# Reordering the small steps beside a deformable convolution: bursts last in their step, sums and statistics earlier, eleven gathers

## The chip, the cores and the metric

The kernel runs on one core of a Trainium2 chip. The metric is the device time of one execution in microseconds; where several runs are given, their median. The engines are named as the profile names them: PE is TensorE (PEld its weight loads), DVE is VectorE, ACT is ScalarE, POOL is GpSimd (here it only issues gathers), SP is SyncE (here it only issues transfers).

## The reference, cut to what matters

Eight images of 256 channels and 64 x 64 points in f32 go through two layers. Each is x + layer(group norm(x)).

```python
def layer0(x):                       # local attention, 4 heads, 3x3 windows
    q, k, v = split(einsum('oc,bchw->bohw', w_qkv, x))
    attn = softmax(sum_d(q * patches(k)))             # 9 weights a head and point
    kernel = grouped_1x1(w_kg, qkv) + b_kg            # 9 more weights, generated
    out = alpha * sum_k(kernel * patches(v)) + beta * sum_k(attn * patches(v))
    return einsum('oc,bchw->bohw', w_proj, out)

def layer1(x):                       # modulated deformable 3x3 convolution
    om = conv3x3(x, w_off) + b_off                    # 18 offsets and 9 masks a point
    v = mask * bilinear(x at the 9 shifted positions) # 4 corners for each
    return einsum('bckhw,ock->bohw', v, w)
```

## The kernel before

A *chunk* is 8 rows of an image, 512 points; an image has 8. The kernel writes out the order of every instruction by hand (`manual_schedule`) for PE, ACT, DVE and POOL; each engine's queue runs in that order. SP's transfers are ordered by what they depend on.

**Slots.** The convolution of layer 1 runs in slots, one for each of the 9 kernel positions of a chunk: 72 an image, 576 in all. Its work is in blocks of 128 points, four a slot. POOL gathers a block's four corners for 256 channels (`gather`, line 764) into one of GATHERS = 10 buffers; ACT scales the first corner (`scale`, 780); DVE adds the other three with three instructions (`sum_corners`, 788). PE transposes the four blocks (`transposes`, 815), ACT copies the result out (818), and PE multiplies it with the weights a slot later (`product`, 832). The product of the 9 slots of a chunk stays in one accumulator `po`, which has a single buffer. After the last of them DVE adds it to the residual r (`finished`, 843) and SP stores it. `ahead(i)` scales blocks i+8 and i+9, sums blocks i+6 and i+7 and issues two gathers; it is called twice a slot. In the last image it issues them four blocks later (LAST_GATHERS = 6).

**Steps.** Everything else is cut into 73 steps an image, which generators yield: two for the first norm, 7 for each of the 8 chunks of attention, 6 that finish the attention and its norm, and 9 for `prepare`, which writes the table to gather from, computes offsets (649), positions (682 to 715) and, for the next image, the first norm's statistics (258). Steps of image b+1 lie beside the slots of image b. Before the first slot, image 0's 73 steps and 6 more run alone; after that each slot is joined by one step (73 for 72 slots), until all are done about 78 slots before the end. A slot's order is: transposes, `ahead`, the product of the slot before, the step, the final sums if the product was a chunk's last, `ahead`.

**A chunk's attention.** In `attention` (550), `a_` is the current chunk and `d` the one before, which is finished beside it. The seven steps are:
1. `spread_weights` of d (475; DVE multiplies the four results, 483), both halves of `q` (276, ACT copies 284);
2. `k` (308) of 10 rows of 66 columns, written in two pieces of 4 rows;
3. `products` (64 small multiplies, 346; DVE masks, 354), first `weighted` half of d (516);
4. `logits` (365 to 374), `keys(1)` of d (498), `generated` (381), `softmax_1` (412, 413, ACT's exponential 414);
5. `v(0)` (308), second `weighted` half, `turned` (398; DVE adds the bias, 402), `softmax_2` (419 to 421), `normed` for the next chunk (228);
6. `v(1)`, `project(0)` (528) and its `add` (539), `softmax_3` (428 to 450);
7. `project(1)` and `add`, `second_stats` (543), `weights` (462), `keys(0)`.

PSUM tiles of the steps come from a ring of four (`psum_a`, 189): each new tile takes the place of the one four before it, once that has been read. `Norm` (195) aggregates statistics on DVE (199) and multiplies the means on PE (201) in one step; `ready` (209) does the variance and the root in the next.

Of the kernel before, what the change touches and what calls it, by code (L numbers as in the profile page):

```python
# [17 lines left out]
P = 128  # L18
C = 256
# [31 lines left out]
GATHERS = 10  # L51
LEAD = SCALE_AHEAD + GATHERS
LAST_GATHERS = 6
# [5 lines left out]
def preact_kernel(ctx: ExitStack, tc: tile.TileContext, a: dict, out: bass.AP):  # L59
# [77 lines left out]

    kt = const.tile([P, NT, R + 2, WP], F32, tag="k", name="k")
    vt = const.tile([P, NT, TC, KT, KT], F32, tag="v", name="v")


    w_effT = const.tile([P, NT, HEADS, KK], F32, tag="w_effT", name="w_effT")
    nc.vector.tensor_scalar(bkg, bkg, alpha, None, ALU.mult)
    with (
        tc.tile_pool(name="prep", bufs=1) as prep,
        tc.tile_pool(name="prep_ps", bufs=1, space=PSUM) as prep_ps,
    ):
        ps = prep_ps.tile([P, NT, HEADS, KK], F32, tag="eff", name="eff")
        for ct in range(NT):
            for h in range(HEADS):  # L150
                for i in range(2):
                    nc.tensor.matmul(
                        ps[:, ct, h, :],
                        w_qkv[h // 2][:, 2 * (h % 2) + i, ct * P : (ct + 1) * P],
                        w_kgT[:, 2 * h + i, :],
                        start=(i == 0),
                        stop=(i == 1),
                    )
        for ct in range(NT):
            nc.vector.tensor_scalar(  # L160
                w_effT[:, ct], ps[:, ct], alpha, None, ALU.mult
            )

        zero = prep.tile([P, ES], F32, tag="zero", name="zero")
        nc.vector.memset(zero, 0.0)
        tables = []  # L170
        for i in range(min(2, B)):
            t = dram.tile([ENTRIES, ES], F32, tag=f"table{i}", name=f"table{i}")
            tables.append(t)
            nc.sync.dma_start(t[:WP], zero[:WP])
            for o in range(H * WP, ENTRIES, P):
                n = min(P, ENTRIES - o)
                nc.sync.dma_start(t[o : o + n], zero[:n])
# [6 lines left out]
    wp = ctx.enter_context(tc.tile_pool(name="wp", bufs=NC + 3))  # L184
# [7 lines left out]
    class Norm:  # L192


        def __init__(self, stats, name):
            self.name = name
            mv = p1.tile([P, NT, 2], F32, tag="mv", name=f"mv_{name}")
            for ct in range(NT):
                nc.vector.bn_aggr(mv[:, ct, :], stats[:, ct].rearrange("p c s -> p (c s)"))
            ps = psum_a(f"gn_{name}")  # L200
            nc.tensor.matmul(ps[:, 0:NT], gmat, mv[:, :, 0], start=True, stop=True)
            self.gn = gn = p2.tile([P, 2, NT], F32, tag="gn", name=f"gn_{name}")
            nc.vector.tensor_copy(gn[:, 0, :], ps[:, 0:NT])
            self.d = d = p1.tile([P, NT], F32, tag="gnd", name=f"gnd_{name}")
            nc.vector.tensor_sub(d, mv[:, :, 0], gn[:, 0, :])
            nc.vector.tensor_mul(d, d, d)
            nc.vector.tensor_add(d, d, mv[:, :, 1])
# [44 lines left out]
    stats0: dict = {}  # L252

    def first_stats(b, c):
        if c == 0:
            stats0[b] = p2.tile([P, NT, NC, 6], F32, tag="stats0", name=f"stats0_{b}")
        for ct in range(NT):
            nc.vector.bn_stats(
                stats0[b][:, ct, c, :], image[:, ct, c * N : (c + 1) * N]
            )  # L260

    class Attention:
# [38 lines left out]
        def keyed(self, which, i, to):  # L301

            for lo, hi in [(0, 2)] * (self.c == 0 and i == 0) + [(2 + 4 * i, 6 + 4 * i)]:
                for m in range(NT):
                    ps = psum_a(f"ps{'qkv'[which]}_{self.u}_{lo}_{m}")
                    o = which * C + m * P
                    for ct in range(NT):
                        nc.tensor.matmul(  # L308
                            ps[:, : (hi - lo) * WP],
                            w_qkvT[:, ct, o : o + P],  # L310
# [4 lines left out]
                    to(m, lo, hi, ps)  # L315

        def k(self, i):
            self.keyed(
                1,
                i,  # L320
                lambda m, lo, hi, ps: nc.scalar.copy(  # L321
                    kt[:, m, lo:hi, :].rearrange("p r w -> p (r w)"), ps[:, : (hi - lo) * WP]
                ),
            )

        def v(self, i):
            self.keyed(
                2,
                i,
                lambda m, lo, hi, ps: nc.scalar.copy(vt[:, m, :, lo:hi, :], tiled(ps, hi - lo)),  # L330
            )

        def products(self):


            self.qk = qk = p1.tile([P, NB, NT, 2, NK], F32, tag="qk", name=f"qk_{self.u}")
            for jj in range(NB // 2):
                both = [psum_a(f"qk_{self.u}_{jj}_{h}") for h in range(2)]
                for ct in range(NT):
                    for j in range(2):  # L340
                        for t in range(2):
                            o = 2 * (2 * jj + j) + t
                            for h in range(2):
                                r = slice(64 * h, 64 * h + 64)
                                n = (2 * j + ct) * NK
                                nc.tensor.matmul(  # L346
                                    both[h][64 * t : 64 * t + 64, n : n + NK],
                                    self.qt[r, ct, o * T * T : (o + 1) * T * T],
                                    kt[r, ct, :, T * o : T * o + KT],
                                    start=True,  # L350
                                    stop=True,
                                )
                for h in range(2):
                    nc.vector.tensor_mul(  # L354
                        qk[:, 2 * jj : 2 * jj + 2, :, h, :],
                        both[h][:, : 4 * NK].rearrange("p (j c k) -> p j c k", j=2, c=NT),
                        near_k.unsqueeze(1).unsqueeze(1).to_broadcast([P, 2, NT, NK]),
                    )
# [17 lines left out]
        def generated(self):  # L376

            ps = psum_a(f"gen_{self.u}")
            n = HEADS * KK
            for ct in range(NT):  # L380
                nc.tensor.matmul(
                    ps[:n],
                    w_effT[:, ct].rearrange("p h k -> p (h k)"),
                    window(self.xn, ct, 4),
                    start=(ct == 0),
                    stop=(ct == NT - 1),
                )
            self.gs = gs = p1.tile([P, N], F32, tag="gs", name=f"gs_{self.u}")[:n]
            nc.scalar.copy(
                gs.rearrange("p (t y x) -> p y t x", y=T, x=T),  # L390
                ps[:n].rearrange("p (y t x) -> p y t x", y=T, x=T),
            )

        def turned(self):
            ps = psum_a(f"gt_{self.u}")
            n = HEADS * KK
            for j in range(NB):
                nc.tensor.transpose(
                    ps[:, j * n : (j + 1) * n], self.gs[:, j * P : (j + 1) * P], ident[:n, :n]
                )  # L400
# [3 lines left out]
                ps[:, : NB * n].rearrange("p (j k) -> p j k", j=NB),  # L404
# [145 lines left out]
    def attention(b):  # L550

        xt = image
        gn = Norm(stats0.pop(b), f"0_{b}")
# [5 lines left out]
        d = None  # L559
        for c in range(NC):  # L560
            a_ = Attention(b, c, xn, stats)
            if d:
                d.spread_weights()
            a_.q(0)
            a_.q(1)
# [3 lines left out]
            yield None  # L569
            a_.products()  # L570
# [3 lines left out]
            a_.logits()  # L574
# [4 lines left out]
            a_.softmax_1()  # L579
            a_.carry_k()  # L580
            yield None
            a_.v(0)
            if d:
                d.weighted(1)
            a_.turned()
            a_.softmax_2()
# [3 lines left out]
            a_.v(1)  # L590
            if d:
                d.add(0, d.project(0))
            a_.softmax_3()
# [4 lines left out]
            a_.weights()  # L598
            a_.keys(0)
            yield None  # L600
            d = a_
# [9 lines left out]
        d.second_stats()  # L611
        yield None
        gn = Norm(stats, f"1_{b}")
# [3 lines left out]
    def prepare(b, gn):  # L617
# [24 lines left out]
        def offsets(c, xn):  # L642
# [14 lines left out]
            om = p1.tile([P, N], F32, tag="gs", name=f"om_{b}_{c}")  # L657
# [134 lines left out]
    def ahead(i):  # L792
# [4 lines left out]
        first = (B - 1) * BLOCKS  # L797
        for n in (i + LEAD, i + LEAD + 1):
            if n < first:
                gather(n)  # L800

        for n in (i + LEAD, i + LEAD + 1):
            if n - GATHERS + LAST_GATHERS >= first:
                gather(n - GATHERS + LAST_GATHERS)

# [48 lines left out]
    with tc.manual_schedule(engines=ordered):  # L854
# [4 lines left out]
        while done < STEPS + STEPS_AHEAD:  # L859
# [15 lines left out]
        for n in range(B * SLOTS + 1):  # L875
            if n < B * SLOTS:
                transposes(*divmod(n, SLOTS))
                ahead(NB * n)
            last = None
            if n > 0:  # L880
                b, h = divmod(n - 1, SLOTS)
                product(b, h)
                if h % KK == KK - 1:
                    last = b, h // KK
            while (done - STEPS - STEPS_AHEAD) * SLOTS < (n + 1) * STEPS:
                next(steps, None)
                done += 1
            if last:
                finished(*last)
            if n < B * SLOTS:  # L890
# [79 lines left out]
```

## Time and profile before

| | us |
|---|---|
| median of 9 runs | 5189.31 (5174.74 to 5207.84) |
| the profiled execution | 5177.06 |
| its span | 5175.3 |
| DVE busy, 0 to 340 / 340 to 4690 / 4690 to the end | 177.7 / 3603.1 / 403.6 |
| PE busy, the same | 273.4 / 4038.9 / 414.9 |
| ACT waits for gathers (line 780 <- DMA) | 434.6 in all, 226.4 in the middle part, 208.2 in the last |
| DVE waits for ACT's scaling (788 <- 780) | 395.5 |

The costliest groups of the page are, with busy us and mean ns: the corner sums on DVE (788) 2799.5 and 479, the convolution's product on PE (832) 2149.1 and 610, the scaling on ACT (780) 1080.6 and 510, the transposes on PE (815) 695.2 and 284. An f32 matmul counts as two instructions (4608 for 2304 products), and a mean of one runs past the start of the next, so times here are taken from start to start. `us, times, longest` follow each pair of engine and releaser in the view of waits. PEclk is the granted clock of PE in tenths.

### The profile page before, as it was taken

The numbers are of one execution on the slowest core, as the hardware profiler recorded it, in microseconds if no ns is written. First come the engines' busy times: TensorE is split into PE (matmuls) and PEld (weight loads), VectorE is DVE, ScalarE is ACT, GpSimd is POOL, SyncE is SP. The second block draws the span as 40 slices with busy tenths as digits, with TensorE's granted clock in tenths as the row PEclk, the third lists the DMA queues.
The fourth block names the chain that finished last, engine by engine and source line by source line (L and its number), as shares of the span: only waits on it lengthen the run. The fifth ranks groups of instructions, "written<-read, shape, count | busy, mean of one in ns | idle before, by whom it ended". The sixth has DMA issues, their size and how long they took to land. (4 is left out here: it accounts for less than half of the span.)

```text
span 5175.3 us, 79716 instructions
## 1 busy us (share of the span) xinstructions
PE 4727.2 (91%) x26592; PEld 2634.4 (51%) x26592; DVE 4184.3 (81%) x10071; ACT 2362.3 (46%) x5184; POOL 3177.1 (61%) x2310
## 2 busy tenths in 40 slices
PE   6979999999999999899998999899999999998888
PEld 4545554555545555455554555445554455544443
DVE  4558787888878888788888888878888887877887
ACT  2334444444444444444444444445444444444544
POOL 0027666666656666566665766757666666666776
PEclk9989999999999999999999999999999999999999
DMA  2058778877787777977779787888878877788998
GB/s 91 21 181 281 266 272 297 305 273 261 273 313 282 273 261 263 332 265 275 277 262 327 270 281 263 285 303 290 273 257 306 300 275 261 272 294 318 380 377 336
DMA packets 476840, 1422.60 MB, mean 275 GB/s; under 512 B 46910, under 2 KB 114750, under 8 KB 476300
## 3 DMA queue, kind: packets, MB, share of 16 engines
q0 software_dynamic: 331776, 1208.11, 66.3%
q1 hardware_dynamic: 141902, 204.27, 11.1%
q10 hardware_dynamic: 2750, 5.12, 0.3%
q8 instruction: 210, 3.44, 0.3%
q14 instruction: 202, 1.65, 0.1%
HBM read 1280.19 MB, written 137.13 MB: 274 GB/s over the span
## 5 line engine op out<-in xcount | busy, mean ns | idle before, releaser
L764 POOL DMA_INDIRECT g<-table,idx x2304 | 3174.6, 1378 | 1976.5 <-DVE s L788 651.0
L788 DVE SCALAR_TENSOR_TENSOR s<-g,wt,s 128x256 f32<-128x256 f32 x6912 | 2799.5, 479 | 404.2 <-ACT s L780 395.5
L832 PE MATMUL po<-vt,w_conv 128*128 128x512 f32 x4608 | 2149.1, 610 | 94.1 <-DVE r L843 94.1
L832 PEld LDWEIGHTS po<-vt,w_conv 128*128 128x128 f32 x4608 | 858.5, 197 | 977.0 <-issue 871.5
L780 ACT ACTIVATE s<-g,wt 128x256 f32<-128x256 f32 x2304 | 1080.6, 510 | 492.2 <-DMA g<-table,idx 434.6
L815 PE MATMUL pt<-ident,s 128*128 128x128 f32 x4608 | 695.2, 284 | 110.4 <-DVE s L788 74.2
L815 PEld LDWEIGHTS pt<-ident,s 128*128 128x128 f32 x4608 | 520.0, 143 | 408.8 <-ACT vt L818 117.5
L818 ACT COPY vt<-pt 128x512 f32<-128x512 f32 x1152 | 610.9, 582 | 119.8 <-PE pt L815 119.4
L276 PE MATMUL psq<-xn,w_qkvT 128*128 128x512 f32 x512 | 284.3, 705 | 91.4 <-DVE wk L483 88.2
L284 ACT COPY q<-psq 128x512 f32<-128x512 f32 x128 | 75.0, 586 | 509.0 <-PE psq L276 509.0
L649 PE MATMUL om<-xn,w_off 128*32 128x512 f32 x2304 | 295.4, 610 | 10.9 <-DVE pos L682 10.8
L308 PE MATMUL psv<-xn,w_qkvT 128*128 128x264 f32 (+1 forms) x1088 | 260.4, 384 | 0.0
L354 DVE TENSOR_TENSOR qk<-qk,near_k 128x400 f32<-128x400 f32 x256 | 129.2, 567 | 161.2 <-PE qk L346 161.2
L308 PE MATMUL psk<-xn,w_qkvT 128*128 128x264 f32 (+1 forms) x1088 | 245.5, 379 | 0.0
L308 PEld LDWEIGHTS psv<-xn,w_qkvT 128*128 128x128 f32 x1088 | 201.6, 192 | 83.2 <-issue 50.6
L276 PEld LDWEIGHTS psq<-xn,w_qkvT 128*128 128x128 f32 x512 | 109.5, 224 | 263.2 <-DVE wk L483 146.1
L528 PE MATMUL proj<-acc,w_projT 128*128 128x512 f32 x512 | 238.2, 592 | 0.7 <-ACT acc L523 0.7
L308 PEld LDWEIGHTS psk<-xn,w_qkvT 128*128 128x128 f32 x1088 | 201.7, 190 | 60.0 <-issue 20.8
L330 ACT COPY v<-psv 128x320 f32<-128x320 f32 (+1 forms) x272 | 110.7, 419 | 255.1 <-PE psv L308 255.0
L321 ACT COPY k<-psk 128x264 f32<-128x264 f32 (+1 forms) x272 | 101.2, 372 | 214.8 <-PE psk L308 214.5
L523 ACT COPY acc<-av 128x512 f32<-128x512 f32 x128 | 74.8, 585 | 254.7 <-PE av L516 254.4
L483 DVE TENSOR_TENSOR wk<-wk,near 100x512 f32<-100x512 f32 x256 | 158.8, 683 | 32.3 <-PE wk L475 32.3
(89 smaller groups left out, 3295.2 us busy)
## 6 DMA issues: line engine op xcount, KB each, us to landing
table<-ts SPq DMA_DIRECT2D x384, 176.0 KB
g<-table,idx POOLq DMA_INDIRECT x2304
x<-in_x_dram SPq DMA_DIRECT2D x64, 512.0 KB
x<-x SPq DMA_DIRECT2D x64, 512.0 KB
r<-x SPq DMA_DIRECT2D x64, 512.0 KB
out_dram<-r SPq DMA_DIRECT2D x64, 512.0 KB
w_conv<-in_w_conv_dram ACTq DMA_DIRECT2D x1, 2304.0 KB
w_qkv<-in_w_qkv_dram ACTq DMA_DIRECT2D x2, 384.0 KB
```

Of the source, the lines that this page charges most:

```text
L276: nc.tensor.matmul(ps, w_qkvT[:, ct, m * P : (m + 1) * P], window(self.xn, ct, 4), start=(ct == 0), stop=(ct == NT - 1),)
L308: nc.tensor.matmul(ps[:, : (hi - lo) * WP], w_qkvT[:, ct, o : o + P], self.xn[:, ct, lo:hi, :], start=(ct == 0), stop=(ct == NT - 1),)
L354: nc.vector.tensor_mul(qk[:, 2 * jj : 2 * jj + 2, :, h, :], both[h][:, : 4 * NK].rearrange("p (j c k) -> p j c k", j=2, c=NT), near_k.unsq ...
L483: nc.vector.tensor_mul(wk.rearrange("p (t n) -> p t n", n=T * T), ps[:NK].rearrange("p (t n) -> p t n", n=T * T), near.unsqueeze(1).to_bro ...
L528: nc.tensor.matmul(ps, w_projT[:, ct, m * P : (m + 1) * P], self.acc[:, ct].rearrange("p (t y x) -> p y t x", y=T, x=T), start=(ct == 0), ...
L649: nc.tensor.matmul(ps[32 * g : 32 * g + 32, :], w_off[:, ct, k, :], window(xn, ct, k), start=(n < 4), stop=(n >= KK * NT - 4),)
L764: nc.gpsimd.indirect_dma_start(out=g, out_offset=None, in_=tables[b % 2], in_offset=bass.IndirectOffsetOnAxis(ap=found[b, c][0][:, j, k : ...
L780: nc.scalar.activation(s, g[:, 0:C], AF.Copy, scale=w[:, 0:1])
L788: nc.vector.scalar_tensor_tensor(s, g[:, q * C : (q + 1) * C], w[:, q : q + 1], s, ALU.mult, ALU.add)
L815: nc.tensor.transpose(pt[ct][:, j, :], s[:, ct * P : (ct + 1) * P], ident)
L818: nc.scalar.copy(v[:, ct, :], pt[ct].rearrange("p b n -> p (b n)"))
L832: nc.tensor.matmul(po[:, m, :], w_conv[:, ct, k, m * P : (m + 1) * P], v[:, ct, :], start=(k == 0 and ct == 0), stop=(k == KK - 1 and ct = ...
```

## The change

- The steps of a chunk are put together anew: (1) `q(1)`, then spreading; (2) `k`, then the first weighted half; (3) `keys(1)`, `generated`, the first half of the products; (4) `v(0)`, the second half of the products, `normed`; (5) `v(1)`, `turned`, the second weighted half, `logits`, `softmax_1`; (6) `project(0)`, `add`, `keys(0)`, `softmax_2`, `softmax_3`; (7) `project(1)`, `add`, statistics, `q(0)` of the next chunk, `weights`.
- `k` is computed for 64 columns, all 8 rows in one tile of 512; its border is set to zero once. The generated weights use all 128 columns of the array (zeros in w_effT); their tile now shares a buffer with `wsb` and `om`.
- In a chunk's last slot the second `ahead` and the final sums stand before the step.
- The aggregation of a norm's statistics stands at the end of the step that completes them; the means (`means`) follow in the next.
- GATHERS is 11, in the last image too. Before the first slot 73 steps run, not 79; the 6 are made up over the first image's slots.

```diff
-GATHERS = 10
+GATHERS = 11
-LAST_GATHERS = 6
...
+    nc.gpsimd.memset(kt, 0.0)
...
+    w_effT = const.tile([P, NT, P], F32, tag="w_effT", name="w_effT")
+    nc.vector.memset(w_effT, 0.0)
...
-    wp = ctx.enter_context(tc.tile_pool(name="wp", bufs=NC + 3))
+    wp = ctx.enter_context(tc.tile_pool(name="wp", bufs=NC + 2))
...
+        if c == NC - 1:
+            norm0[b] = Norm(stats0[b], f"0_{b}")
...
+        def k(self, m):
+            for lo, hi in [(0, 2)] * (self.c == 0) + [(2, R + 2)]:
+                ps = psum_a(f"psk_{self.u}_{lo}_{m}")
+                for ct in range(NT):
+                    nc.tensor.matmul(
+                        ps[:, : (hi - lo) * W],
+                        w_qkvT[:, ct, C + m * P : C + (m + 1) * P],
+                        self.xn[:, ct, lo:hi, 1 : W + 1],
...
         for c in range(NC):
-            a_ = Attention(b, c, xn, stats)
+            a_.q(1)
             if d:
                 d.spread_weights()
-            a_.q(0)
-            a_.q(1)
             yield None
             a_.k(0)
             a_.k(1)
-            yield None
-            a_.products()
             if d:
                 d.weighted(0)
             yield None
-            a_.logits()
             if d:
                 d.keys(1)
                 d.carry_v()
             a_.generated()
-            a_.softmax_1()
-            a_.carry_k()
+            a_.products(0)
             yield None
             a_.v(0)
-            if d:
-                d.weighted(1)
-            a_.turned()
-            a_.softmax_2()
+            a_.products(1)
+            a_.carry_k()
             if c + 1 < NC:
                 xn = normed(xt, gn, c + 1)
             yield None
             a_.v(1)
+            a_.turned()
+            if d:
+                d.weighted(1)
+            a_.logits()
+            a_.softmax_1()
+            yield None
             if d:
                 d.add(0, d.project(0))
+            a_.keys(0)
+            a_.softmax_2()
             a_.softmax_3()
             yield None
             if d:
                 d.add(1, d.project(1))
                 d.second_stats()
-            a_.weights()
-            a_.keys(0)
+            d = a_
+            if c + 1 < NC:
+                a_ = Attention(b, c + 1, xn, stats)
+                a_.q(0)
+            d.weights()
             yield None
-            d = a_
...
         d.second_stats()
+        gn = Norm(stats, f"1_{b}")
         yield None
-        gn = Norm(stats, f"1_{b}")
+        gn.means()
         yield None
         yield gn.ready()
...
-        first = (B - 1) * BLOCKS
-        for n in (i + LEAD, i + LEAD + 1):
-            if n < first:
-                gather(n)
-
-        for n in (i + LEAD, i + LEAD + 1):
-            if n - GATHERS + LAST_GATHERS >= first:
-                gather(n - GATHERS + LAST_GATHERS)
+        gather(i + LEAD)
+        gather(i + LEAD + 1)
...
-        while done < STEPS + STEPS_AHEAD:
+        while done < STEPS:
...
         for n in range(B * SLOTS + 1):
+            last = None
+            if n > 0 and n % KK == 0:
+                last = divmod(n // KK - 1, NC)
             if n < B * SLOTS:
                 transposes(*divmod(n, SLOTS))
                 ahead(NB * n)
-            last = None
+                if last:
+                    ahead(NB * n + 2)
             if n > 0:
-                b, h = divmod(n - 1, SLOTS)
-                product(b, h)
-                if h % KK == KK - 1:
-                    last = b, h // KK
-            while (done - STEPS - STEPS_AHEAD) * SLOTS < (n + 1) * STEPS:
+                product(*divmod(n - 1, SLOTS))
+            if last:
+                finished(*last)
+
+            goal = (n + 1) * STEPS + min(n + 1, SLOTS) * STEPS_AHEAD
+            while (done - STEPS) * SLOTS < goal:
                 next(steps, None)
                 done += 1
-            if last:
-                finished(*last)
-            if n < B * SLOTS:
+            if n < B * SLOTS and not last:
                 ahead(NB * n + 2)
```

## The prediction

> **What bounds the kernel now.** I read the busy shares first, then who waits for whom, then the order in time on two engines. From the page:
>
> ```profile
> PE 4727.2 (91%) x26592; PEld 2634.4 (51%) x26592; DVE 4184.3 (81%) x10071; ACT 2362.3 (46%) x5184; POOL 3177.1 (61%) x2310
> PEclk9989999999999999999999999999999999999999
> ```
>
> TensorE works 91% of the span at almost full clock; VectorE is second at 81%. The span has three parts: up to 340 us (no slots), 340 to 4690 (slots with steps beside them), 4690 to the end (slots alone). What TensorE waits for in the middle part is the whole question:
>
> ```profile
> PE psq L276 <- DVE wk L483: 88.2, 49, 2.2
> PE po L832 <- DVE r L843: 88.0, 40, 4.5
> PE gn L201 <- DVE mv L199: 49.5, 14, 5.6
> PE pt L815 <- DVE s L788: 29.2, 79, 6.5
> PE pt L815 <- ACT vt L818: 22.1, 12, 3.2
> ```
>
> (Engine, line, releaser: us, times, longest.) The first three are what the change moves: queries behind spreading, the product of a new chunk behind the final sums, the means behind the aggregation. A wait also costs clock. Busy time by stretch, with the granted clock after POOL's column:
>
> ```profile
> 2000.00:2005.00 5.00, 4.71 (x7) 2.02 (x8) 4.40 (x10) 0.58 (x1) 4.39 (x3) 0.66 0.85 293
> 2005.00:2010.00 5.00, 5.00 (x19) 2.70 (x18) 2.49 (x6) 3.15 (x7) 3.78 (x5) 1.00 0.81 261
> ```
>
> At 2000 us TensorE had just waited 2.21 us; the clock is 0.66 in the next 5 us. So a wait is priced with its slow stretch.
>
> Then the order in time, TensorE (start, duration) and VectorE:
>
> ```profile
> 2000.29 5.40 PE L276 MATMUL psq<-xn,w_qkvT 128*128 128x512 f32 x8 [2.21 <-DVE wk L483]
> 2020.49 1.09 PE L815 MATMUL pt<-ident,s 128*128 128x128 f32 x8
> 2024.85 1.04 PE L498 MATMUL vk<-ident,v 128*100 128x128 f32 x8
> 2210.75 0.59 PE L201 MATMUL gn<-mv,gmat 128*128 128x2 f32 x2 [5.58 <-DVE mv L199]
> ```
>
> ```profile
> 1994.81 4.82 DVE L788 SCALAR_TENSOR_TENSOR s<-g,wt,s 128x256 f32<-128x256 f32 x12
> 1999.55 2.48 DVE L483 TENSOR_TENSOR wk<-wk,near 100x512 f32<-100x512 f32 x4
> 2205.36 4.83 DVE L788 SCALAR_TENSOR_TENSOR s<-g,wt,s 128x256 f32<-128x256 f32 x12
> 2210.09 0.60 DVE L199 BATCH_NORM_AGGREGATE mv<-stats 128x2 f32<-128x48 f32 x2
> ```
>
> A slot's transposes and products cost TensorE 4.36 us (2020.49 to 2024.85); its twelve corner sums cost VectorE 4.82. In steps without a wait, start to start on TensorE: queries 3.44 for two, spreading 1.05, keys of the window 3.56, small products 1.6, a weighted half 1.1, the turned keys (vk) 0.97, generated 1.84, a value half 1.8, a projection 1.72, weights 0.44. One chunk is 7 slots of 4.36 plus 23.5, so 54 us; VectorE's is 7 x 4.82 plus 15.9 of step work plus 1.29 for final sums every 9 slots, so 51 to 52. Chunks really take about 59.3 (queries at 2333 and 2632, five chunks apart, are 299 us apart, over 59 each). TensorE is the bound by a margin of 3 us in 54: **VectorE is next, close behind**.
>
> **Part by part**, against the profiled execution (span 5175.3, time 5177.06; the median shown is 5189.31, 12 higher; I add the sum to the median). The middle part holds images 1 to 7, 56 chunks.
>
> *Queries before spreading.* 88.2 us of waiting go. Their slow stretches too: the queries' matmuls there are busy 251.7 us for 448, 0.562 each; unhindered (94.42 to 97.97 in the first part) eight take 3.55, 0.444 each; 0.118 x 448 = 53. So -141. What is late next: the fourth spreading product needs the fourth buffer of the ring of four, which ScalarE empties of the query (0.586 us) while TensorE does three spreadings (0.8); with a hand-over about 0.2 x 56 = +11 (between 0 and one copy, +33).
>
> *Final sums before the step.* 88.0 us of waiting go; 28 of the 40 are above 2 us, each with 53/49 = 1.1 us of slow clock as above: 31. So -119. What comes back: in a chunk's last slot VectorE now does twelve corner sums (4.82), the sums on r (1.29), then the step. Below I count by which step they meet.
>
> *Statistics forward.* The wait of 5.58 at 2210.75 looks free to take. But the twelve corner sums of 2205.36 to 2210.1 stand ahead of the aggregation, and the transposes behind gn need the last six of them. With the aggregation earlier, gn starts at 2206 and the transposes stop till 2210.7. The 49.5 us mostly change their name: about 0.6 to 0.9 gained in each of 14, -10. (Bounds: 0 and -50 with clock.)
>
> *Small products, softmax and statistics spread.* TensorE's work only changes place. VectorE's step work per chunk was 2.5, 0, 2.0, 3.7, 2.0 to 2.5, 3.5, 1.9; it becomes 2.5, 0, 1.0, 2.1, 4.0 (bias, logits, first softmax), 4.45 (add, rest of the softmax), 1.9. Steps five and six cost TensorE 7.8 and 7.0 with their slots, VectorE 8.8 and 9.3: it falls 3.3 us behind. How much TensorE feels: step four ends in a burst whose products VectorE must multiply, so both meet at zero there. VectorE then needs 1.0, 1.1 (normed), 4.8, 4.0, 4.8 before it has finished the corner sums that the transposes of step seven need: 15.8 against TensorE's 14.8 plus 0.4 of first transposes, a wait of 0.7. Step six's 4.45 and 4.8 more: 25.1 against 24.2, 1.0. Later steps catch up (step two has no VectorE work). So 1.7 a chunk, **+95** (bounds: 0 if my zero is off by a microsecond, and 3.3 a chunk, +185).
> With final sums in the slot, the same count with 1.29 and six corner sums moved ahead gives an extra wait of about 2.7, 1.0, 0, 0.6, 1.2, 2.1, 3.6 us as they meet steps one to seven: 1.6 on average. 43 of the 56 fall on attention steps: 69, with 6 for the others **+75**. Three in seven are above 2 us: 18 x 1.1 = **+20** of slow clock. Behind a late VectorE, ScalarE's exponential holds the scales and the evacuation of pt; counted as above, pt is empty 1.5 us before it is needed, so nothing.
>
> *Keys in 512 columns.* 8 instructions of 0.43 (3.44) for 16 (3.56): -7. ScalarE: 2 x 0.585 for 4 x 0.372, off the path. *Generated and turned at full width:* 1.84 to 1.72 and 0.37 to 0.44, -3. *Bursts apart:* before, products and weighted stood together; one more small-tile visit a chunk. The gap between po and qk at 2017.8 is about 0.1, so +10. Together 0. [...]
> [...]
>
> *Eleven gathers, eleven in the last image too.* Middle: ScalarE waits 226.4 us there for gathers, but TensorE feels 22.1 of it (pt <- vt); between 0 and -22 (up to +10 if tables written at the same time land later), taken -15. Last part: DMA share 0.92, 356 GB/s, while 398 occurs at 2075: at best -50; r and the output share the engines with five more gathers, 7 us each for 8 chunks, at worst +55. Taken -10.
>
> *Six steps fewer ahead of the first slot.* gather(0) waits for the last positions (338.43) before as after. The first transposes come at 365.5 now, since VectorE, ScalarE and TensorE do four attention steps first; without them some 16 us earlier, but those 17 us of TensorE work then lie in image 0's slots. Nothing, +-10. Memsets (about 1.2 and 0.5 us by rows L136, L131) lie in the load.
>
> **Sum.** -141 +11 -119 -10 +95 +75 +20 +0 -15 -10 = **-94**: 5189 - 94 = **5095** (profile: about 5083).
>
> **Rivals.**
> 1. *VectorE keeps up.* If its delay is absorbed, only the 11 comes back: -141 -119 -10 +11 -25 = -284, **4905**. For it: pt <- s is only 29.2 us now, and VectorE's idle in the middle part is 4350 - 3603 = 747. Against: it runs without a pause from 2043.4 to 2068.
> 2. *Given back entirely*, the waits only renamed as with gn: returns near 5 us a chunk, **5190**, within 0.3%, about what a measurement of this kernel can tell from no change.
> 3. *The softmax lump decides: slower.* The delay of steps five and six is felt whole, 3.3 a chunk instead of 1.7 (+90), with a slow stretch each (56 x 1.1 = +62): **5247**. It decides once new stalls and their clock exceed 295/56 = 5.3 us a chunk. For it: both engines have nearly equal loads, and steps five and six hold 8.4 of 15.9. Against: step two gives VectorE 4 us to recover.
>
> **Chances.** Forecast 0.55 (4990 to 5160), rival 1 0.20, rival 2 0.12 (a little of it still faster), rival 3 0.13. Faster 0.77, same 0.10, slower 0.13. The range 4900 to 5205 takes in half of rival 1 and all of rival 2.
>
> **What would show it.** psq <- wk gone and psq's mean near 610 ns: the first step right. po <- r smaller but alive, at 2 to 3.6 us: the second. gn <- mv gone with new waits of 4 to 5 us at pt beside it: the third. pt <- s grown from 29 to above 100 us, VectorE without idle from step five to one, idle in steps two to four: the fourth. If pt <- s stays near 30, rival 1 holds. I am wrong if ScalarE or the gathers become what VectorE waits for (s <- s above 336), or if the last part is longer than 485.

## The result, and the profile after

The changed kernel takes **5217.15 us** (median of 10 runs, 5203.05 to 5236.81); the kernel before 5184.22 (31 runs). The ratio is **1.0065** (95% interval 1.0051 to 1.0079): 0.65% slower, clear of the noise, where 0.98 was forecast. The profiled execution has a span of 5205.5 us.

Its page, the busy time of the engines:

```profile
PE 4776.9 (92%) x26080; PEld 2577.3 (50%) x26080; DVE 4177.1 (80%) x10072; ACT 2372.4 (46%) x5056; POOL 3329.7 (64%) x2311
```

TensorE has 512 matmul instructions fewer to do and is busy 50 us longer; its mean granted clock is 0.966 against 0.967, so over the whole span no slow clock was gained. It went from the queries, as meant (the page's rows before and after), but the rows of the projection rose from 592 to 616 ns in the mean and those of the convolution's product from 610 to 617:

```profile
L276 PE MATMUL psq<-xn,w_qkvT 128*128 128x512 f32 x512 | 284.3, 705 | 91.4 <-DVE wk L483 88.2
L286 PE MATMUL psq<-xn,w_qkvT 128*128 128x512 f32 x512 | 244.0, 601 | 1.6 <-DVE xn L235 1.6
```

What TensorE waits for between 340 and 4690 us:

```profile
PE pt L820 <- DVE s L799: 117.1, 128, 11.7
PE po L837 <- DVE r L848: 75.9, 42, 3.4
PE qk L354 <- ACT vk L508: 30.9, 16, 3.5
PE proj L533 <- ACT acc L528: 20.9, 7, 3.4
PE ptab L640 <- DVE xn L235: 17.2, 14, 2.5
PE w L467 <- DVE wts L455: 16.3, 7, 3.4
```

psq and gn are gone from the list, as the change meant. But all lines together are 308 us, against 314 before: **the waits changed their names**. po <- r, which was 88, stands at 76; qk, proj and w are new.

Where in a chunk the time lies is seen from the start of each slot's first transposes. Mean length of a slot by its place in the chunk, images 1 to 6 (place 0 holds the final sums of the chunk before, place 1 begins the new chunk's product):

| place | 0 | 1 | 2 | 3 | 4 | 5 | 6 | 7 | 8 | sum |
|---|---|---|---|---|---|---|---|---|---|---|
| before | 9.42 | 10.43 | 7.12 | 9.47 | 7.87 | 8.77 | 8.11 | 8.58 | 8.76 | 78.5 |
| changed | 9.74 | 10.65 | 8.24 | 8.84 | 8.17 | 8.44 | 8.56 | 8.26 | 8.21 | 79.1 |

Places 0 and 1, which the new order of final sums was to shorten, are longer, and place 2 by most. And the first image: slot 0 begins 15.8 us earlier than before (349.7 against 365.5), slot 72 begins 16.6 us later (1005.4 against 988.8).

One last slot shows what keeps po. VectorE and then TensorE, in order of time; step seven lies in the slot that ends at 2583.45, the final sums in the next:

```profile
2580.03 7.21 DVE L799 SCALAR_TENSOR_TENSOR s<-g,wt,s 128x256 f32<-128x256 f32 x18
2587.16 1.28 DVE L848 TENSOR_TENSOR r<-po,r 128x512 f32<-128x512 f32 x2
```

```profile
2583.45 0.60 PE L820 MATMUL pt<-ident,s 128*128 128x128 f32 x4
2584.52 0.83 PE L820 MATMUL pt<-ident,s 128*128 128x128 f32 x4 [0.47 <-DVE s L799]
2588.49 6.25 PE L837 MATMUL po<-vt,w_conv 128*128 128x512 f32 x8 [3.14 <-DVE r L848]
```

VectorE comes late out of the softmax and has 18 corner sums in a row before it: 6 left over from the slot before the last, then the last slot's 12, six of which the change has put here. Only then does it free po. TensorE waits 3.14 us, and its next product takes 6.25 instead of 3.70, at a granted clock of 0.59. This is one of the worst cases: of the 42 products after such a wait 18 are lengthened, by 2.0 us in the mean, 36 us in all; the other 24 take 3.70.

The longest waits at pt between two images come from elsewhere: there VectorE waits for a load of x, and its corner sums stand behind that.

```profile
3487.59 1.29 DVE L266 BATCH_NORM_STATS2 stats<-x 128x6 f32<-128x512 f32 x2 [9.05 <-DMA x<-in_x_dram]
3490.99 1.09 PE L820 MATMUL pt<-ident,s 128*128 128x128 f32 x4 [5.03 <-DVE s L799]
```

These waits of VectorE for x are 76.1 us in the middle part, against 22.0 before.

### The profile page after: what moved, and what is told of

Read it like the earlier page. It is cut to its first block, busy times and chain, and to the rows that moved or that the text cites. A ratio compares the mean times of both kernels' runs of the same rounds, so it can differ in the third digit from the quotient of the medians.

```text
span 5205.5 us, 78551 instructions
## 1 busy us (share of the span) xinstructions
PE 4776.9 (92%) x26080; PEld 2577.3 (50%) x26080; DVE 4177.1 (80%) x10072; ACT 2372.4 (46%) x5056; POOL 3329.7 (64%) x2311
## 4 chain that ended last, share of the span: by engine, by line
PE 42%; DVE 34%; DMA 17%; issue 4%; ACT 2%; POOL 1%; SPq 0%; DVEq 0%; ACTq 0%; POOLq 0%
DVE s L799 19%; PE po L837 17%; DMA g<-table,idx 11%; PE pt L820 4%; PE psk L315 4%; DMA x<-in_x_dram 4%; PE psv L332 3%; PE psq L286 2%; PE qk L354 2%; PE om L660 2%; DMA table<-ts 2%; DVE xn L235 2%; PE wk L480 2%; DVE by L373 2%; PE gen L388 1%
## 5 line engine op out<-in xcount | busy, mean ns | idle before, releaser
L775 POOL DMA_INDIRECT g<-table,idx x2304 | 3326.0, 1444 | 1855.1 <-DVE s L799 643.3
L837 PE MATMUL po<-vt,w_conv 128*128 128x512 f32 x4608 | 2174.7, 617 | 102.1 <-DVE r L848 102.1
L820 PE MATMUL pt<-ident,s 128*128 128x128 f32 x4608 | 711.5, 286 | 146.2 <-DVE s L799 132.6
L533 PE MATMUL proj<-acc,w_projT 128*128 128x512 f32 x512 | 250.5, 616 | 26.3 <-ACT acc L528 26.3
L286 PE MATMUL psq<-xn,w_qkvT 128*128 128x512 f32 x512 | 244.0, 601 | 1.6 <-DVE xn L235 1.6
L315 PE MATMUL psk<-xn,w_qkvT 128*128 128x512 f32 (+1 forms) x576 | 238.1, 558 | 0.3
L322 ACT COPY k<-psk 128x512 f32<-128x512 f32 (+1 forms) x144 | 78.0, 552 | 266.3 <-PE psk L315 266.3
L646 ACT COPY ts<-ptab 88x512 f32<-88x512 f32 x192 | 106.6, 584 | 167.2 <-DMA table<-ts 133.7
L533 PEld LDWEIGHTS proj<-acc,w_projT 128*128 128x128 f32 x512 | 98.8, 197 | 150.5 <-issue 108.2
L660 PEld LDWEIGHTS om<-xn,w_off 128*32 128x32 f32 x2304 | 74.9, 111 | 186.6 <-issue 160.6
```

The costliest lines, as they stand in the source:

```text
L286: nc.tensor.matmul(ps, w_qkvT[:, ct, m * P : (m + 1) * P], window(self.xn, ct, 4), start=(ct == 0), stop=(ct == NT - 1),)
L315: nc.tensor.matmul(ps[:, : (hi - lo) * W], w_qkvT[:, ct, C + m * P : C + (m + 1) * P], self.xn[:, ct, lo:hi, 1 : W + 1], start=(ct == 0), ...
L533: nc.tensor.matmul(ps, w_projT[:, ct, m * P : (m + 1) * P], self.acc[:, ct].rearrange("p (t y x) -> p y t x", y=T, x=T), start=(ct == 0), ...
L660: nc.tensor.matmul(ps[32 * g : 32 * g + 32, :], w_off[:, ct, k, :], window(xn, ct, k), start=(n < 4), stop=(n >= KK * NT - 4),)
L775: nc.gpsimd.indirect_dma_start(out=g, out_offset=None, in_=tables[b % 2], in_offset=bass.IndirectOffsetOnAxis(ap=found[b, c][0][:, j, k : ...
L820: nc.tensor.transpose(pt[ct][:, j, :], s[:, ct * P : (ct + 1) * P], ident)
```

## The experiments

Eighteen runs in five sets, each on a chip of its own. The chips fall into two kinds. Where the result above and the third set were measured, the kernel before takes about 5180 us; on the other four chips it takes 5535 to 5553, and a slot without steps takes 7.4 to 8.0 us instead of 5.6 to 5.8. Ratios are to the kernel before on the same chip; I call the chips quick and slow. The changed kernel itself was not run beside the third set, so what is said there against it is across two chips of the quick kind (kernel before: 5184 and 5179 us).

The theories: **A**, parts of the change cost, each by itself (the order of the last slot, the six steps, spreading's wait for the query's copy); **B**, the new grouping with VectorE's delay after steps five and six is the cost; **C**, eleven gathers hold up other transfers.

**First set: one part undone** (slow chip, no run of the changed kernel beside).

*undo_steps*: 79 steps ahead again.

```diff
-        while done < STEPS:
+        while done < STEPS + STEPS_AHEAD:
...
-            goal = (n + 1) * STEPS + min(n + 1, SLOTS) * STEPS_AHEAD
-            while (done - STEPS) * SLOTS < goal:
+            while (done - STEPS - STEPS_AHEAD) * SLOTS < (n + 1) * STEPS:
```

> The changed kernel with 79 steps run before the first slot again; all else as changed. Kernel before 5184, changed kernel 5217. Theory A (parts of the change cost, each by itself: six steps moved beside the slots of image 0, scales that stand before their gathers have landed in a chunk's last slot, the spreading products' wait for the query's copy): slot 72 of the changed kernel comes 17 us later than before although its first slot comes 16 us earlier, so this gives some 15 us back, about 5200. Theory B (the new grouping of the steps is the cost, VectorE's delay after steps five and six): the six steps cost what they cost anywhere, within 3 us of 5217.

*undo_final*: final sums and second ahead behind the step.

```diff
-                if last:
-                    ahead(NB * n + 2)
...
-            if last:
-                finished(*last)
...
-            if n < B * SLOTS and not last:
+            if last:
+                finished(*last)
+            if n < B * SLOTS:
```

> The changed kernel with the final sums and the second ahead of a chunk's last slot behind the step again, as before. Theory A: in last slots ScalarE's wait for gathers falls from 147 to some 30 us and the waits of qk for vk and of proj for acc (52 us) go; po behind r returns to about 90. Net gain 25 to 45, about 5180. Theory B: the final sums are no loss where they stand, and their old place costs the wait of po again: 5217 to 5240.

*sums_early*: only the second ahead behind the step.

```diff
-                if last:
-                    ahead(NB * n + 2)
...
-            if n < B * SLOTS and not last:
+            if n < B * SLOTS:
                 ahead(NB * n + 2)
```

> The changed kernel with only the second ahead of a chunk's last slot behind the step again; the final sums stay before the step. Theory A: the scales are what is early, not the sums: as good as or better than the run with both behind, 5165 to 5180, with po behind r well under 76 us. If the place of the final sums themselves costs, it stays near 5217. Theory B: within 5 us of 5217.

*undo_gathers*: 10 gathers, 6 in the last image (the diff of the change, backwards).

> The changed kernel with 10 gathers, 6 in the last image, as before. Theory A: eleven gathers are a gain, 15 us of it in the last image (the lag on the kernel before falls from 46 to 31 us there), so this is about 5232 or more. Rival C (a deeper queue of gathers holds up the loads of x and the table writes: VectorE's wait for x rose from 22 to 76 us in the middle part, ScalarE's for table writes from 92 to 132): the slots between images get 3 to 5 us shorter each, about 5200.

| | ratio | interval |
|---|---|---|
| undo_steps | 1.0160 | 1.0139 to 1.0181 |
| undo_final | 1.0152 | 1.0133 to 1.0171 |
| sums_early | 1.0139 | 1.0117 to 1.0160 |
| undo_gathers | 1.0153 | 1.0132 to 1.0175 |

The times can't be set against 5217 and lie within each other's intervals, so no verdict by time. The trace shows the waits: po <- r (340 to 4900 us) is 63.0 us in undo_steps, which has the new order, 136.2 in undo_final and 5.1 in sums_early. With the new steps the old place of the final sums makes TensorE wait longer than the new; without the second ahead in front of them the wait is gone. Theory C finds nothing in undo_gathers: VectorE still waits 58.9 us for loads of x between 340 and 4690 (60.1 in undo_steps).

**Second set: the changed kernel as measure** (slow chip).

> The changed kernel itself, as the common measure: the chip of the last four runs needs 7.4 to 8.0 us for a slot without steps, where the chip of the kernel before and of the changed kernel needs 5.7 to 5.8, so those four can't be set against 5217. Both theories: 1.0065 of the kernel before if the chip moves gathers as fast as the first (5.7 us a slot in the last part), some 1.015 if it is as slow as the second.

> 79 steps before the first slot, all else as changed. Theory A: 15 us less than the changed kernel on the same chip, since slot 72 came 17 us late with 73. Theory B: within 3 us of it.

> Only the second ahead of a chunk's last slot behind the step again; final sums stay early. Theory A (scales that stand before their gathers have landed hold ScalarE, and with it vk, acc and the products that need them): ScalarE's wait for gathers in last slots falls from 147 to below 60 us, the waits of qk for vk and proj for acc (52 us in the middle part) go; 25 to 45 us less than the changed kernel. Theory B: within 5 us of it.

*q_in_seven*: both halves of q in step seven.

```diff
         a_.q(0)
+        a_.q(1)
         for c in range(NC):
-            a_.q(1)
...
                 a_.q(0)
+                a_.q(1)
             d.weights()
```

> The changed kernel with both halves of q in step seven, so that step one is spreading alone and its four results find tiles of the ring that were read long before. Theory A: the four spreading products take 1.05 us again instead of 1.84 (the fourth waited for the query's copy), 0.75 x 56 chunks = 42 us less work on TensorE; but step one leaves TensorE 5.4 us beside VectorE's 7.3 and step seven becomes 10.3, so a part comes back as waits of pt for s: 10 to 35 us less than the changed kernel. Theory B (VectorE is the bound in steps five to one): no gain, pt behind s grows by as much as the spreading gains, within 5 us.

| | us | ratio | interval |
|---|---|---|---|
| after_again | 5636.15 | 1.0180 | 1.0156 to 1.0203 |
| undo_steps_2 | 5628.25 | 1.0164 | 1.0139 to 1.0188 |
| sums_early_2 | 5599.98 | 1.0105 | 1.0084 to 1.0127 |
| q_in_seven | 5652.70 | 1.0212 | 1.0185 to 1.0240 |

sums_early_2 is 36 us below the changed kernel, the expected size, intervals apart (the fourth set shows that the reason expected there, early scales, was not it). The six steps are not told from nothing here. In q_in_seven the four spreadings take 1.05 us again (1.77 in the changed kernel, median of 64), as expected, and yet it is not faster: pt <- s is 193 us against 182, qk <- vk 55 against 44. There B was right: the waits for VectorE and ScalarE grew by about what the spreadings gained.

**Third set: parts alone** (quick chip).

*q_alone* and *sums_alone* are the kernel before with one part each (the changed kernel has only one half of q ahead of the spreading in step one, q_alone has both):

```diff
-            if d:
-                d.spread_weights()
             a_.q(0)
             a_.q(1)
+            if d:
+                d.spread_weights()
```

```diff
+            if last:
+                finished(*last)
             while (done - STEPS - STEPS_AHEAD) * SLOTS < (n + 1) * STEPS:
                 next(steps, None)
                 done += 1
-            if last:
-                finished(*last)
```

> The kernel before, with one part of the change alone: in step one both halves of q come ahead of the spreading. Theory A: the 88 us that psq waits for wk and the slow clock behind them (53) go; the fourth spreading product then waits some 0.75 us for the query's copy (42 us in all), and a part comes back as waits for VectorE: 0.985 to 0.995 of the kernel before. Theory B (VectorE is the bound in these slots, its delay only changes its name): 0.995 to 1.0, pt behind s up by 60 us or more.

> The kernel before, with another part alone: the final sums stand before the step, the second ahead stays behind it. Theory A: po behind r (88 us and 31 us of slow clock) goes nearly whole, since VectorE reaches the sums after six corner sums (2.45 us) and the product of the slot's own accumulator, and nothing is early on ScalarE: 0.985 to 0.995. Theory B: VectorE waits for the product instead (1.9 us each) and gives it back to pt: 0.998 to 1.003.

*grouping_alone* is the changed kernel with undo_steps, undo_final and undo_gathers together; *best_after* the changed kernel with undo_steps and sums_early.

> The new steps alone (with the keys in 512 columns, the full width and the statistics forward); the order of a chunk's last slot, the 79 steps ahead and the gathers as before. Theory A: the steps themselves are no loss, slots two to eight of a chunk are as fast or faster: 0.990 to 1.002. Theory B (the grouping is what makes the changed kernel slow): as slow as the changed kernel, 1.005 or more.

> The changed kernel with 79 steps ahead and with the second ahead behind the step; final sums early. Theory A: both gains add, 30 to 55 us below the changed kernel, so 0.996 to 1.001 of the kernel before on a chip with quick gathers, some 1.009 on one with slow ones. Theory B: no more than 10 us below the changed kernel.

| | us | ratio | interval |
|---|---|---|---|
| q_alone | 5094.97 | 0.9833 | 0.9809 to 0.9856 |
| sums_alone | 5138.55 | 0.9922 | 0.9901 to 0.9942 |
| grouping_alone | 5234.87 | 1.0105 | 1.0084 to 1.0126 |
| best_after | 5061.55 | **0.9770** | 0.9748 to 0.9793 |

Two parts of the change are gains alone; the grouping alone is a loss, as B said; and the grouping, the early sums and the gathers, with the second ahead and the six steps put back, **beat both kernels** by 118 and about 155 us, far more than the 30 to 55 that I expected against the changed kernel. In grouping_alone po <- r is the largest wait of all (136.6 us from 340 to 4690), with the sums behind the heavy steps; with the sums early, in best_after, the grouping does no harm that shows. That it gains anything is not shown: the two parts alone multiply to 0.9756, which lies within best_after's interval. In best_after, over the same stretch:

```profile
PE pt L820 <- DVE s L799: 129.8, 165, 4.2
PE proj L533 <- ACT acc L528: 20.5, 7, 3.5
PE ptab L640 <- DVE xn L235: 19.4, 14, 3.0
PE w L467 <- DVE wts L455: 16.7, 7, 2.6
PE gn L208 <- DVE mv L203: 9.8, 6, 5.1
PE qk L354 <- ACT vk L508: 8.5, 20, 1.1
PE om L660 <- DVE pos L693: 7.9, 6, 3.1
PE po L837 <- DVE r L848: 6.5, 10, 0.8
```

po <- r falls from 76 to 6.5, qk <- vk from 31 to 8.5; the clock rises from 0.966 to 0.976. The same last slot as above, VectorE and TensorE:

```profile
2507.23 4.83 DVE L799 SCALAR_TENSOR_TENSOR s<-g,wt,s 128x256 f32<-128x256 f32 x12
2511.98 1.28 DVE L848 TENSOR_TENSOR r<-po,r 128x512 f32<-128x512 f32 x2
```

```profile
2511.72 0.83 PE L820 MATMUL pt<-ident,s 128*128 128x128 f32 x4 [0.46 <-DVE s L799]
2513.32 3.70 PE L837 MATMUL po<-vt,w_conv 128*128 128x512 f32 x8 [0.76 <-DVE r L848]
```

Twelve corner sums instead of 18, a wait of 0.76 instead of 3.14, and the product in 3.70 us instead of 6.25. From slot 72 to slot 498, where the two kernels differ in nothing but the order of the last slot, best_after needs 3632.9 us and the changed kernel 3743.2, 110 less; places 0 and 1 alone fall from 9.74 and 10.65 to 9.28 and 8.76, and the other seven cancel out. On the slow chip of the second set the same edit (sums_early_2) gains as much at places 0 to 2 (28.64 us against 31.02), but over these slots only 46 us (3945.4 against 3991.2): places 4 to 6 are longer there. Theory C falls too: with eleven gathers VectorE's wait for loads of x is 27.7 us in best_after. It is 54 to 76 us in all eight kernels with the early corner sums, whatever the number of gathers, and 11 to 34 in the other twelve; why, the runs don't show.

**Fourth set: which half of the second ahead** (slow chip). *corner_early* leaves only its corner sums in front of the final sums, *scales_early* only its scales:

```diff
                 if last:
-                    ahead(NB * n + 2)
+                    sum_corners(NB * n + 2 + SUM_AHEAD)
```

```diff
                 if last:
-                    ahead(NB * n + 2)
+                    scale(NB * n + 2 + SCALE_AHEAD)
+                    scale(NB * n + 3 + SCALE_AHEAD)
```

with the rest of that ahead behind the step.

> The changed kernel, in a chunk's last slot: of the second ahead only the corner sums stand before the final sums, its two scales and gathers stand behind the step. Changed kernel 1.0065 of the kernel before on a quick chip; with the second ahead whole behind the step and 79 steps 0.977. Theory A1 (VectorE's order: six corner sums, 2.45 us, ahead of the final sums keep the accumulator of the next chunk's product occupied): po behind r stays near 76 us, and the time near 1.0065, at least 0.998. Theory A2 (ScalarE's order: scales that wait for gathers hold its other work): po behind r falls with the rest, 0.985 or less.

> The changed kernel, in a chunk's last slot: of the second ahead only the two scales stand early, its corner sums and gathers behind the step. Theory A1: po behind r below 15 us, 0.985 or less. Theory A2: ScalarE's wait for gathers in last slots stays near 147 us, qk behind vk and proj behind acc near 52 us, time 0.998 or more. If both halves are needed (VectorE's sums follow ScalarE's scales), both kernels land between 0.985 and 0.998.

> 79 steps before the first slot, all else as changed, on a quick chip if it is one. From the slots' times: 17 us below the changed kernel, 1.003 of the kernel before. If the six steps cost nothing where they are, 1.0065.

> The changed kernel with the second ahead whole behind the step, 73 steps as changed. On a quick chip: the run with 79 steps and this gave 0.977; less some 0.003 for the steps this is 0.980. If the steps matter more beside it, up to 0.985.

| | us | ratio | interval |
|---|---|---|---|
| corner_early | 5613.74 | 1.0090 | 1.0058 to 1.0121 |
| scales_early | 5588.21 | 1.0046 | 1.0022 to 1.0070 |
| undo_steps_3 | 5613.26 | 1.0092 | 1.0057 to 1.0128 |
| sums_early_3 | 5602.00 | 1.0069 | 1.0047 to 1.0091 |

By time, scales_early is the faster by 26 us, though the intervals overlap a little (from slot 72 to 498: 3935.7 against 3984.0 us). sums_early_3 is 11 us below undo_steps_3, which has the early corner sums, within the intervals. The waits over the whole span decide; of corner_early, then of scales_early:

```profile
PE po L838 <- DVE r L849: 77.4, 40, 8.0
```

```profile
PE po L838 <- DVE r L849: 8.4, 13, 0.8
```

**A1 holds** for the wait: it is VectorE's order, six corner sums in front of the sums that free the accumulator. What I had taken for the cause first, ScalarE held by gathers, is not what keeps po; qk <- vk is 16.1 and 20.0 us in the two, against 5.5 in sums_early_3, so neither half alone makes that wait. The times that A1 and A2 named were for a quick chip and are not tested.

**Fifth set** (slow chip). *q_and_sums* is the kernel before with both diffs of q_alone and sums_alone.

> The changed kernel with the second ahead of a chunk's last slot whole behind the step, 73 steps as changed. On a chip with quick gathers: between the changed kernel's 1.0065 and the 0.977 of the run that has the 79 steps too. If VectorE's order in the last slot is the main cost, 0.978 to 0.983; if the six steps are, 0.995 or more. On a chip with slow gathers about 1.007 to 1.014, as it was.

> The kernel before with two parts of the change and nothing else: both halves of q before the spreading, and the final sums before the step, the second ahead behind it. Alone they gave 0.983 and 0.992. If each frees TensorE of its own wait, 0.970 to 0.977, the fastest kernel here; if VectorE's delay takes part of it back, 0.977 to 0.983. On a chip with slow gathers nearer to 1, 0.985 to 0.995, since there the gathers bound the slots.

sums_early_4 gave 5592.86, 1.0099 (1.0062 to 1.0136), q_and_sums 5654.66, **1.0210** (1.0178 to 1.0242): the opposite of the sign that its parts have on the quick chip, and outside the 0.985 to 0.995 expected; that the gathers bound the slots there was my estimate. Its TensorE in one step three:

```profile
2514.71 1.49 PE L346 MATMUL qk<-k,q 64*64 64x100 f32 x49
2516.53 0.40 PE L346 MATMUL qk<-k,q 64*64 64x100 f32 x4 [0.32 <-issue]
2517.25 0.24 PE L346 MATMUL qk<-k,q 64*64 64x100 f32 x1 [0.32 <-issue]
2517.97 0.40 PE L346 MATMUL qk<-k,q 64*64 64x100 f32 x4 [0.48 <-issue]
2519.37 0.41 PE L346 MATMUL qk<-k,q 64*64 64x100 f32 x4 [1.01 <-issue]
2520.80 0.49 PE L346 MATMUL qk<-k,q 64*64 64x100 f32 x2 [1.02 <-issue]
```

"issue" is idle time for which the profile shows no releaser. After some fifty small products TensorE stops and starts; that slot takes 13 to 18 us in every chunk, where the kernel before, on the quick chip, takes 6.0 to 7.1. Neither part was run alone on a slow chip, so which of them brings it, or whether the kernel before has it there too, is open, and so is whether q and sums add up on a quick chip.

## Why the prediction was wrong, point by point

The forecast was -94 us; the measured move is +33, 127 more.

**The step that failed is the price of a wait**: each wait was taken off together with the slow stretch behind it (53 and 31 us of slow clock), as if neither came back elsewhere, only 20 us of slow clock were put beside the returning waits (none beside the 95 us at pt), and the waits behind ScalarE at nothing. In the runs the waits between 340 and 4690 us are 308 us for 314, where the sum has 31 less, and the granted clock stayed (0.966 for 0.967), where the sum has 64 us of slow clock less. The two parts alone say the same: queries first is worth 84 us where the sum counts 141 - 11 = 130, early final sums 41 where it counts 119. Together that is 124 short, nearly the whole miss (which may be luck, as q_alone is not quite the change's part). In sums_alone po <- r falls from 88.0 to 5.3 us, but psq <- wk rises from 88.2 to 107.8 and the clock falls from 0.967 to 0.963.

Term by term:

- **Queries before spreading**: the waiting of 88 did go, and 42 of the 53 of slow clock (psq busy 251.7 to 210.0; the 53 sets a busy time of 0.562 against a start-to-start time of 0.444). The +11 for spreading's wait is mis-sized, and past its upper bound of 33: the four spreadings take 1.77 us instead of 1.05, 56 x 0.72 = 40. It hides in TensorE's busy time (spreading's rows: 62.6 us to 98.1).
- **Final sums before the step**, "-119 ... +75 ... +20": the returning wait was foreseen in mechanism and size (75 and 75.9). Its clock was not: 36 us of lengthened products (37 before), where 31 were to go and 20 to return. The six corner sums moved forward were priced at 95 and cost 110 by best_after; the price was near, but I took the order of the last slot as one edit, where it was two: sums_alone shows that the early final sums are a gain (0.9922), corner_early that the corner sums in front of them bring the wait back.
- **"Behind a late VectorE, ScalarE's exponential holds ... so nothing"**: failed. qk <- vk 31 and proj <- acc 21 are new, 52 us; w <- wts 16, released by VectorE, was not counted either.
- **Statistics forward**: gn <- mv (49.5) is gone, as forecast. But the waits of 4 to 5 us at pt that were to be its sign are those for x; some 19 us of pt <- s stand behind the moved aggregations. In best_after gn <- mv is 9.8 again. What this part is worth was not measured by itself.
- **Steps five and six**, +95 on pt <- s: the total is near by luck. It rose from 29 to 117, but counted by what VectorE did just before, 42 us stand behind the softmax (13 before), 34 behind the statistics that wait for x (none before), 19 behind the aggregations and 12 at the very first slot (6.5 before).
- **Six steps fewer ahead**, "nothing, +-10": the first 72 slots cost 32 us more and begin 16 us earlier, so up to +17, the order of the last slot included. No run on a quick chip separates this from the rest of the change; on the slow chip it was 8 us with overlapping intervals.
- **Eleven gathers**: in the middle pt <- vt fell from 22 to 1 (21.4 in grouping_alone, with ten). In the last image the lag falls from 46 us to 31 between slots 480 and 575, but that this is the gathers is not shown: on the third set's chip these slots take 607.5 to 614.6 us with the old number and 613.1 with eleven.
- *Bursts and widths*, 0: rather a loss. In the middle part the small products' busy time rose from 91.6 to 114.0 and turned from 24.4 to 33.6, while psk fell only from 214.8 to 207.7 and generated from 107.1 to 105.9: some 23 us more in these rows together.

The signs that the prediction named nearly all came (psq's mean 601 ns, po <- r smaller but alive, gn <- mv gone, pt <- s above 100), and yet the time moved the other way: apart from psq's mean they look at waits, and none at the clock or at busy time as a whole.

Of the rivals, the second is nearest in mechanism (given back entirely, the waits only renamed), the third had the right side: slow clock did come with the new waits (after 3.43 us behind acc at 1468.39 the projection's eight matmuls take 6.51 us at a clock of 0.56, where eight without a wait, at 85.51 in the kernel before, take 3.60 at 1.00), but the softmax's delay, 42 us, is far below the 185 that it needs. VectorE's order decides at the accumulator (po <- r 77.4 us in corner_early, 8.4 in scales_early), and best_after keeps the softmax steps. At po the length of a wait told only in part whether it cost clock: of the 42 waits there all eight above 3 us were followed by a lengthened product, ten of the 26 between 1 and 2.6 us and none of the eight below 0.5.

## What to carry to other kernels

Where an engine's order is written by hand, the operations that free a single-buffered accumulator must stand in front of work that merely runs ahead; moving both forward together gives the gain away (po <- r was 88 us before, 5.3 in sums_alone, 76 in the changed kernel). A wait that goes need not take its slow clock along (psq's 88 us went, and the granted clock is 0.966 for 0.967): look where the next wait will stand, and price slow clock there as well. One lengthened instruction is no price either; here 18 of 42 were. And try the parts of a change one by one: here two parts gained 1.7% and 0.8%, and on the quick chips one misplaced `ahead` cost about 110 us and turned the whole into a loss.

## What the runs showed of the hardware

Chips differ by more than the change: 5165 to 5208 us against 5515 to 5596 for the same kernel. What else their other cores did meanwhile is not on record. The last part of the changed kernel, on a quick and on a slow chip (the last two columns are the share of the DMA engines and GB/s, before them the clock):

```profile
4900.00:5100.00 200.00, 179.91 (x573) 86.96 (x574) 177.41 (x433) 102.08 (x212) 157.62 (x140) 0.93 0.99 389
```

```profile
5300.00:5500.00 200.00, 143.55 (x436) 72.10 (x435) 136.50 (x332) 75.74 (x163) 142.14 (x106) 0.85 0.77 292
```

On the slow one a quarter fewer bytes move (292 against 389 GB/s), at a lower share (0.77 against 0.99), so the DMA engines are not full there. The second difference is TensorE's idle time without a releaser: 80 to 278 us in the profiles of the slow chips, none in those of the quick ones. Most of it stands before pt, po and qk in the kernels with the new steps, and in the bursts of small products in q_and_sums (qk 161.2, av 88.7). The two may have one cause; the runs don't show it. The number of gathers in flight decides little: a slot without steps (510 to 570) takes 5.57 to 5.80 us on the quick chips with six in the last image and 5.68 and 5.69 with eleven; on the slow ones 7.37 (undo_gathers) and 7.60 (q_and_sums) with six and 7.55 to 8.02 with eleven. A part's price, then, holds for the kind of chip that it was measured on.
